# A scan mixer laid out by channel halves in place of even and odd rows

## The chip, the cores and the metric

The kernel runs on one core of a Trainium2 chip, as one launch. The metric is the device time of a whole execution in microseconds, given as the median of several runs; lower is better. A separate execution of the same kernel was profiled, and every busy time, wait and start below is from that one.

## The reference

The input is 32 images of 56 × 56 tokens of 96 channels. Two layers follow one another. Layer 0 adds shifted-window attention (7 × 7 windows, 3 heads) and then a feed-forward product in fp8 (96 → 384 → 96). Layer 1 adds a gated scan along the width and then a second feed-forward product. The change is in the scan mixer of layer 1, which computes this:

```python
x_n   = layernorm(layernorm_c(x))                   # 96 channels
u     = x_n @ W_expand                              # 192 channels
gate  = sigmoid(x_n @ W_gate)                       # 192 channels
# along the width w, for each row and channel e:
state = state * A + u[w] * B                        # 16 states
y[w]  = sum(state * C) + 16 * u[w] * D
out   = x + (gate * y) @ W_out                      # 192 -> 96
```

The recurrence is linear with constant coefficients, so for one channel `y = T_e u`, where `T_e` is a 56 × 56 lower triangular Toeplitz matrix of the channel's taps. The kernel computes the taps once, lays the 192 matrices out in SBUF, and then does the scan as matrix products.

## The kernel before

**Tiles and rounds.** An image is four blocks of 14 rows; a block is 7 tiles (`G`) of two rows, so 112 tokens. A block passes through about a hundred named steps, each an instruction or a few on one engine. The function `pipeline` is written out at build time: in round `t` it goes through a table such as `PIPELINED`, and an entry `name:lag` issues step `name` for block `t - lag`. So about eleven blocks are in flight, and the order of instructions on each engine is exactly the order of the table; every engine runs its own in order. There are three tables: `FILL` for the first 7 rounds, `PIPELINED`, and `DRAIN` for the last ones. The steps `SC` and `GA` work on whole images and are issued in every fourth round only.

**Steps by engine.** TensorE: `q`, `k`, `v` (projections), `sc` (scores), `av` (attention output), `tro`, `pr` (its output projection), `ta`, `tf`, `te`, `tg` (transposes of normalized tiles), `hf0..2`, `yf`, `hg0..2`, `yg` (feed-forward), and of the mixer `pu0..3`, `SC0..5`, `gt0..1`, `so`. VectorE: statistics and normalizations (`s*`, `n*`), `st*` (score scaling), `rc`, `ad`, `as`, `rf*`, `rg*`, `c*`, and `GA0..5`. ScalarE: copies out of PSUM (`e*`, `x*`, `z*`), the exponentials `ex0..2`, `th0..3` and `uc0..3`. GpSimd: the powers `p*`, `k*`, `cf1`, `cg1` and `r0`. SyncE: loads `LD` and stores `ST`. All PSUM tiles come from one pool of four tiles of two banks each, so the fifth tile waits until the first has been read out.

**The mixer before.** The scan needs the position along the width on the partitions. Step `xe` (line 810) writes the transposed tile into `xs`, 96 channels by three rows of 64 columns; `r0` (line 820) copies the first row to the third place. `pu` (lines 831 and 832) takes two rows at once as the stationary operand, 128 columns, so that the even row's tokens come out on partitions 0 to 63 and the odd row's on 64 to 127. It streams 288 columns of the weights over rows 0 and 1, and the last 96 over rows 1 and 2, which puts the second half of the expanded channels on the other half of the partitions. `th` (line 839) writes half the argument's tanh into `gts`, `uc` (line 844) the expanded values into `u`; both hold 128 partitions × 28 row pairs × 192 channels.

`SC` (line 855) multiplies: for each channel and each parity one product of a 64 × 64 piece of `toep` with the 28 rows of that parity of the image. Four such products of 64 × 64 use the four quarters of the array. A step makes 64 of them, `UNIT` = 16 channels of either half, and there are six steps an image. `GA` (line 870) forms (gate + 1) × y into `gts`. `gt` (lines 887 and 893) transposes back, channels on partitions: 128 channels into `gTa`, and the other 64 into the lower or upper half of `gTb` by the tile's parity; `eg` (line 904) copies them out of PSUM. `so` (lines 912 and 916) does the output product: 7 products over 128 channels and 7 over 64.

**Set-up.** `taps_t` holds the taps, position by channel. `load_toep` writes them 56 times to DRAM and reads them back with a slanted pattern, which gives the Toeplitz matrices with position outermost; both halves of the partitions get all 192 channels, in the buffers `gts`. `turn_toep` (line 309) turns them to channel outermost in `toep`, two copies on VectorE and two on ScalarE, before round `gates`, the lag of `th`.

A condition on the inputs picks between this pipeline and a careful, unpipelined one (`IN_TURN`); the inputs here take the pipeline.

Of the kernel before, what the change touches and what calls it, by code (L numbers as in the profile page):

```python
# [23 lines left out]
C = 96  # L24
HW = 56
# [8 lines left out]
UNIT = 16  # L34
# [4 lines left out]
NRP = NBLK * G  # L39
# [17 lines left out]
    "q:2 SC4:8 pf:3 rg2:10 xg1:10 k:2 nf:3 GA3:8 GA4:8 rg1:10 eq:2 pe:4 hg0:10 ne:4 v:2 SC2:8 cg1:10 "  # L57
    "cg2:10 xg0:10 ek:2 ev:2 tf:3 rg0:10 ef:3 so:9 cg0:10 GA2:8 te:4 sc:2 as:9 xe:4 st1:2 st2:2 ST:11 "
    "r0:4 hf2:3 st0:2 xf2:3 ex1:2 ex2:2 yg:10 zg:10 hf1:3 ex0:2 xf1:3 sg:9 SC0:8 pg:9 rf2:3 bg:10 "
    "GA0:8 pu0:4 th0:4 hf0:3 rf1:3 SC5:8 LD:0 uc0:4 cf1:3 pu1:4 ng:9 GA5:8 av:2 xf0:3 rc:2 pa:1 rf0:3 "  # L60
    "uc1:4 th1:4 gt0:8 eg0:8 tg:9 cf0:3 pu2:4 tro:2 pu3:4 kg:10 cf2:3 eg:9 yf:3 uc2:4 th2:4 sa:0 eo:2 "
    "uc3:4 pr:2 zf:3 na:1 bf:3 th3:4 SC1:7 ad:2 ta:1 GA1:7 gt1:8 hg2:9 ea:1 sf:2 kf:3 eg1:8 hg1:9 "
    "SC3:7 xg2:9 se:3 "
# [4 lines left out]
    "GA0:8 pf:3 q:2 bg:10 eq:2 rg2:10 k:2 v:2 cg0:10 yg:10 pe:4 ek:2 xg2:9 hg2:9 nf:3 tf:3 ev:2 "  # L68
    "rg1:10 ne:4 pa:1 gt0:8 xg0:10 zg:10 sc:2 ng:9 ef:3 eg1:8 eg0:8 st1:2 st2:2 kg:10 eg:9 te:4 hf0:3 "
    "st0:2 hf2:3 so:9 xe:4 xf2:3 ST:11 gt1:8 SC4:8 ex0:2 rf2:3 ex1:2 LD:0 cf2:3 r0:4 ex2:2 pu0:4 "  # L70
    "GA3:8 hf1:3 SC1:7 xg1:10 xf0:3 hg0:10 pu1:4 rf0:3 xf1:3 uc1:4 rf1:3 av:2 tg:9 rg0:10 th0:4 pg:9 "
    "rc:2 uc0:4 GA2:8 cf1:3 th1:4 SC5:8 pu2:4 as:9 tro:2 uc2:4 eo:2 cf0:3 GA5:8 yf:3 GA1:7 na:1 zf:3 "
    "sg:9 pr:2 cg2:10 sa:0 SC2:8 bf:3 GA4:8 ad:2 SC0:8 cg1:10 sf:2 kf:3 hg1:9 th2:4 se:3 SC3:7 pu3:4 "
    "ta:1 uc3:4 ea:1 th3:4 "
# [3 lines left out]
    "pf:3 pe:4 hg0:10 rc:2 nf:3 GA3:8 tf:3 k:2 sf:2 rg2:10 ST:11 ne:4 cg2:10 ex2:2 SC5:8 xg1:10 so:9 "  # L78
    "xg0:10 ef:3 SC2:8 hf1:3 eq:2 rg1:10 cg1:10 te:4 tro:2 rg0:10 cg0:10 LD:0 as:9 xf1:3 xe:4 hf2:3 "
    "r0:4 ea:1 hf0:3 yg:10 st1:2 v:2 ek:2 pr:2 xf2:3 GA5:8 pu3:4 xf0:3 sg:9 ev:2 rf1:3 SC4:8 st0:2 "  # L80
    "st2:2 pu1:4 rf2:3 zg:10 rf0:3 cf0:3 pu0:4 th3:4 th1:4 cf2:3 ad:2 ex1:2 cf1:3 uc1:4 GA2:8 GA4:8 "
    "bg:10 q:2 eo:2 ta:1 SC0:8 uc3:4 uc0:4 pg:9 ng:9 th0:4 GA0:8 yf:3 kg:10 pu2:4 zf:3 gt0:8 uc2:4 "
    "av:2 eg0:8 th2:4 ex0:2 bf:3 tg:9 SC1:7 eg:9 pa:1 sc:2 gt1:8 hg2:9 SC3:7 GA1:7 eg1:8 kf:3 hg1:9 "
    "xg2:9 na:1 se:3 sa:0 "
# [5 lines left out]
    "yf:0 zf:0 bf:0 kf:0 se:0 pe:0 ne:0 te:0 xe:0 r0:0 pu0:0 th0:0 uc0:0 pu1:0 th1:0 uc1:0 pu2:0 th2:0 "  # L90
# [7 lines left out]
def kernel(  # L98
# [73 lines left out]
    weg = zeros(2 * E, "weg")  # L172

# [23 lines left out]

    u = const.tile([128, NRP, E], F32, name="u")
    gts = [const.tile([128, NRP, E], F32, name=f"gt_{n}") for n in range(2)]
    for gt, eng in zip(gts, (nc.vector, nc.gpsimd)):  # L200
        eng.memset(gt, 0.0)
# [76 lines left out]
    nc.vector.tensor_copy(taps_t, pt[0 : 2 * HW, 0, 0:E])  # L278
# [3 lines left out]
    toep = const.tile([128, E * HW + RS - HW], F32, name="toep")  # L282
    nc.vector.memset(toep[:, E * HW :], 0.0)

    def load_toep():


        nc.sync.dma_start(taps_d.rearrange("w j e -> j w e"), taps_t[:, None, :].to_broadcast([2 * HW, HW, E]))
        src = taps_d[:, :, :]
        for half in (0, RS):  # L290

            for w0, w1 in ((0, 48), (48, HW - SH), (HW - SH, HW)):
                for t0, t1 in ((0, NRP), (NRP, HW - SH), (HW - SH, HW)):
                    w_in, w_out = (w0 + SH) % HW, (t0 + SH) % HW
                    first = w_in * 2 * HW + HW - w_in + w_out
                    nc.sync.dma_start(
                        gts[t0 // NRP][half + w0 : half + w1, t0 % NRP : t0 % NRP + t1 - t0].rearrange("w t e -> w (t e)"),
                        bass.AP(
                            tensor=src.tensor,
                            offset=src.offset + first * E,  # L300
                            ap=[[(2 * HW - 1) * E, w1 - w0], [1, (t1 - t0) * E]],
                        ),
                    )

    def turn_toep():
        toep3 = toep[:, 0 : E * HW].rearrange("p (e t) -> p e t", t=HW)
        for e0 in range(0, E, EH):
            for n, copy in enumerate((nc.vector.tensor_copy, nc.scalar.copy)):
                copy(
                    toep3[:, e0 : e0 + EH, n * NRP : (n + 1) * NRP],  # L310
                    gts[n][:, :, e0 : e0 + EH].rearrange("p t e -> p e t"),
                )
# [90 lines left out]
    nc.scalar.dma_start(weg[0:C, 0:E], w_gate)  # L403
    nc.scalar.dma_start(weg[0:C, E : 2 * E], w_expand)
    nc.scalar.dma_start(wso[:, 0], ssm_w_out[0:128])
    for p0 in (0, 64):
        nc.scalar.dma_start(wso[p0 : p0 + 64, 1], ssm_w_out[128:E])


    xws, vs, xqs = [], [], []  # L410
# [12 lines left out]
    gTa = const.tile([128, G, TP], F32, name="gTa")  # L423
    gTb = const.tile([128, (G + 1) // 2, TP], F32, name="gTb")
# [10 lines left out]
    xs = const.tile([128, G, 3, RS], F32, name="xs")  # L435
# [372 lines left out]
    def _(i):  # L808
        for g0, g1, pt in held.pop(("tre", i)):
            nc.scalar.activation(  # L810
                xs[0:C, g0:g1, 0:2, 0:HW],
# [6 lines left out]
    @steps("r0")  # L818
    def _(i):
        nc.gpsimd.tensor_copy(xs[0:C, :, 2, 0:HW], xs[0:C, :, 0, 0:HW])  # L820

    def rows_of(i, j):

        return (i % NBLK) * G + 2 * j, min(2, G - 2 * j)

    @steps("pu0", "pu1", "pu2", "pu3")
    def _(i, j):
        pu = banks(f"pu_{i}_{j}")
        for g in range(rows_of(i, j)[1]):
            rows = xs[:, 2 * j + g].rearrange("c r w -> c (r w)")  # L830
            nc.tensor.matmul(pu[:, g, 0 : E + EH], rows[:, 0:128], weg[:, 0 : E + EH], start=True, stop=True)  # L831
            nc.tensor.matmul(pu[:, g, E + EH : 2 * E], rows[:, RS:], weg[:, E + EH :], start=True, stop=True)  # L832
        held["pu", i, j] = pu

    @steps("th0", "th1", "th2", "th3")
    def _(i, j):
        rp, n = rows_of(i, j)
        gt = gts[i // NBLK % 2]
        nc.scalar.activation(gt[:, rp : rp + n, :], held["pu", i, j][:, 0:n, 0:E], AF.Tanh, scale=0.5)  # L839

    @steps("uc0", "uc1", "uc2", "uc3")
    def _(i, j):
        rp, n = rows_of(i, j)
        nc.scalar.copy(u[:, rp : rp + n, :], held["pu", i, j][:, 0:n, E : 2 * E])  # L844
# [3 lines left out]
    def _(n, s):  # L848
        py = banks(f"scan_{n}_{s}")
        for e in range(UNIT):  # L850
            for p in range(2):
                for eh in range(2):
                    ch = eh * EH + s * UNIT + e
                    o0 = (1 - p if eh else p) * RS
                    nc.tensor.matmul(  # L855
                        py[o0 : o0 + RS, eh, e * NRP : (e + 1) * NRP],
                        toep[p * RS : (p + 1) * RS, ch * HW : ch * HW + RS],
                        u[p * RS : (p + 1) * RS, :, ch],
# [6 lines left out]
    def _(n, s):  # L865
        py = held.pop(("scan", n, s))
        for eh in range(2):
            e0 = eh * EH + s * UNIT
# [5 lines left out]
                py[:, eh, 0 : UNIT * NRP].rearrange("p (e q) -> p q e", q=NRP),  # L874
# [7 lines left out]
    def _(i, k):  # L882
        g0, g1 = halves[k]
        gt = gts[i // NBLK % 2][:, i % NBLK * G : (i % NBLK + 1) * G, :]
        pt = banks(f"gt_{i}_{k}")
        for g in range(g0, g1):
            nc.tensor.transpose(pt[:, 0, (g - g0) * 128 : (g - g0 + 1) * 128], gt[:, g, 0:128], ident)  # L887


        for half in (1, 0):  # L890
            for m in range(2):
                g = min(g0 + 2 * m + half, G - 1)
                nc.tensor.transpose(  # L893
                    pt[0 : 64 + 64 * half, 1, m * 128 : (m + 1) * 128], gt[:, g, 128 - 64 * half : E], ident
                )
# [3 lines left out]
    def _(i, k):  # L899
        g0, g1 = halves[k]  # L900
        pt = held.pop(("gt", i, k)).rearrange("c b (s w) -> c b s w", w=RS)[:, :, :, 0:HW]
        for b, dst in ((0, gTa[:, g0:g1]), (1, gTb[:, 2 * k : 2 * k + 2])):
            dst = dst.rearrange("c g (r w) -> c (g r) w", w=HW)
            nc.scalar.copy(dst, pt[:, b, 0 : dst.shape[1]])  # L904

    @steps("so")
    def _(i):
        po = banks(f"so_{i}")[0:TP]
        dst = lambda g: po[:, g % 2, g // 2 * C : (g // 2 + 1) * C]

        for g in range(G):
            nc.tensor.matmul(dst(g), gTa[:, g, :], wso[:, 0, :], start=(g < 2), stop=False)  # L912

        for g in range(G):
            half = slice(g % 2 * 64, g % 2 * 64 + 64)
            nc.tensor.matmul(dst(g), gTb[half, g // 2, :], wso[half, 1, :], start=False, stop=(g >= G - 2))  # L916
        held["so", i] = []
        for b in range(2):
            n = (G + 1 - b) // 2
# [92 lines left out]
```

## Time and profile before

| | |
|---|---|
| median of 3 runs (3761.55 to 3764.2) | 3763.2 us |
| profiled execution, its own time | 3752.4 us |
| its span | 3750.7 us |
| mean granted TensorE clock | 0.984 |
| scan products, `SC` L855: records, mean duration of one | 24576, 221 ns |
| `pu` L831: records, mean duration of one | 1792, 421 ns |
| `pu` L832: records, mean duration of one | 1792, 261 ns |
| `GA` L870 on VectorE: instructions, mean duration of one | 384, 617 ns |

The page gives the busy time of an engine as the union of its instructions; since matrix products overlap in the array, the mean duration of one says little of what it costs, and the distance between starts says more. Each f32 product appears as two records, each with its own load of weights (PEld). The chain of waits is followed back from the last instruction; the chain between two times gives the pieces of it in that stretch. A row of the timeline merges instructions of one kind that follow one another.

### The profile page before, as it was taken

Reading aid. Unit: us, or ns where it says so; the run is one execution under the profiler, and the core shown is the slowest. Engines: PE = TensorE matmul, PEld = TensorE weight load, DVE = VectorE, ACT = ScalarE, POOL = GpSimd, SP = SyncE. Lnnn points to the kernel's source line nnn. Section 1 sums busy time; section 2 is a strip of 40 time slices with the busy share of each in tenths; the row PEclk is TensorE's granted clock in tenths of the full one; section 3 lists DMA queues with packets and bytes.
Section 4 is the critical chain, followed back from the end, with each engine's and each line's share of the span. In section 5 each row is a group of like instructions: output and inputs, shape, how many; then the busy total and the mean of one; then the engine's idle time right before and its main releaser. Section 6 shows DMA issues by size and latency. Waiting matters only on the chain.

```text
span 3750.7 us, 179098 instructions
## 1 busy us (share of the span) xinstructions
PE 3623.0 (97%) x78756; PEld 3079.2 (82%) x78756; DVE 3140.3 (84%) x9418; ACT 2327.9 (62%) x4867; POOL 1427.9 (38%) x1176
## 2 busy tenths in 40 slices
PE   4999999999999999999999999999999999999996
PEld 3788888888888888888888888888888888888875
DVE  5788888888888888888888888888888888888875
ACT  2666666666666666656666666666666666666662
POOL 2333333443334443334443434443334443334432
PEclk8999999999999999999999999999999999999997
DMA  6001011011001101100101101101011101101000
GB/s 137 17 13 26 23 23 29 22 25 26 22 23 26 25 23 27 23 23 23 29 22 27 24 23 25 26 22 29 23 23 26 25 22 28 23 23 26 22 15 22
DMA packets 226367, 99.42 MB, mean 27 GB/s; under 512 B 218492, under 2 KB 225246, under 8 KB 225358
## 3 DMA queue, kind: packets, MB, share of 16 engines
q1 hardware_dynamic: 222522, 86.81, 10.4%
q8 instruction: 623, 10.21, 1.1%
q10 hardware_dynamic: 3060, 1.08, 0.1%
q14 instruction: 162, 1.33, 0.1%
HBM read 44.47 MB, written 43.35 MB: 23 GB/s over the span
## 4 chain that ended last, share of the span: by engine, by line
PE 94%; DMA 2%; issue 2%; DVE 2%; POOL 1%; ACT 0%; SPq 0%; ACTq 0%; POOLq 0%; DVEq 0%
PE pu L831 12%; PE scan L855 11%; PE qk L550 8%; PE av L674 5%; PE pv L569 5%; PE so L912 5%; PE pr L723 5%; PE pu L832 5%; PE s L592 4%; PE ph_g L743 4%; PE ph_f L743 4%; PE py_f L777 4%; PE py_g L777 3%; PE so L916 3%; PE gt L887 3%; PE tr_o L703 3%
## 5 line engine op out<-in xcount | busy, mean ns | idle before, releaser
L831 PE MATMUL pu<-weg,xs 128*128 128x288 f32 x1792 | 608.5, 421 | 2.4 <-ACT h_f L755 1.2
L799 POOL TENSOR_TENSOR xb<-xb,y_f 112x672 f32<-112x672 f32 x128 | 188.0, 1469 | 782.7 <-DVE y_f L795 782.7
L855 PEld LDWEIGHTS scan<-u,toep 64*64 64x64 f32 x24576 | 385.4, 136 | 83.9 <-issue 59.1
L855 PE MATMUL scan<-u,toep 64*64 64x28 f32 x24576 | 411.0, 221 | 21.4 <-issue 20.3
L832 PEld LDWEIGHTS pu<-weg,xs 128*128 128x128 f32 x1792 | 340.3, 190 | 96.1 <-POOL xs L820 1.9
L755 ACT CAST h_g<-ph_g 128x784 f16<-128x784 f32 x384 | 302.6, 837 | 122.7 <-PE ph_g L743 112.4
L755 ACT CAST h_f<-ph_f 128x784 f16<-128x784 f32 x384 | 316.9, 827 | 76.4 <-PE ph_f L743 70.2
L623 DVE SCALAR_TENSOR_TENSOR pT<-s,bias 128x392 f32<-128x392 f32 (+1 forms) x512 | 213.6, 459 | 142.3 <-PE s L592 137.9
L810 ACT ACTIVATE xs<-tr_e,bet,gam 96x448 f32<-96x448 f32 (+1 forms) x256 | 158.6, 668 | 269.3 <-PE tr_e L499 269.3
L474 POOL TENSOR_TENSOR rs_g<-rs_g,neg_half 112x7 f32<-112x7 f32 x128 | 202.9, 1585 | 319.8 <-DVE rs_g L468 319.8
L870 DVE SCALAR_TENSOR_TENSOR gt<-gt,scan 128x448 f32<-128x448 f32 x384 | 220.9, 617 | 121.5 <-PE scan L855 121.5
L820 POOL COPY xs<-xs 96x392 f32<-96x392 f32 x128 | 65.7, 513 | 673.7 <-issue 662.5
L550 PE MATMUL qk<-xw,wqkv 128*32 128x196 f32 (+1 forms) x3072 | 310.8, 398 | 11.8 <-ACT xw L540 7.6
L832 PE MATMUL pu<-weg,xs 128*128 128x96 f32 x1792 | 320.9, 261 | 0.5 <-POOL xs L820 0.4
L484 DVE TENSOR_SCALAR xn_g<-xb,st_g,rs_g 112x96 fp8e5<-112x96 f32 x896 | 295.6, 397 | 30.2 <-POOL rs_g L474 30.1
L844 ACT COPY u<-pu 128x384 f32<-128x384 f32 (+1 forms) x512 | 233.1, 456 | 115.5 <-PE scan L855 59.9
L831 PEld LDWEIGHTS pu<-weg,xs 128*128 128x128 f32 x1792 | 281.9, 191 | 19.5 <-ACT h_f L755 2.0
L484 DVE TENSOR_SCALAR xn_e<-xb,st_e,rs_e 112x96 f32<-112x96 f32 x896 | 287.9, 390 | 0.2 <-POOL rs_e L474 0.2
L839 ACT ACTIVATE gt<-pu 128x384 f32<-128x384 f32 (+1 forms) x512 | 242.8, 474 | 56.1 <-PE pu L832 56.1
L474 POOL TENSOR_TENSOR rs_f<-rs_f,neg_half 112x7 f32<-112x7 f32 x128 | 201.1, 1571 | 183.4 <-DVE rs_f L468 183.4
L550 PEld LDWEIGHTS qk<-xw,wqkv 128*32 128x32 f32 (+1 forms) x3072 | 117.6, 119 | 165.3 <-issue 69.2
L904 ACT COPY gTa<-gt 128x448 f32<-128x448 f32 (+1 forms) x256 | 125.3, 490 | 193.9 <-PE gt L893 183.7
(151 smaller groups left out, 9015.2 us busy)
## 6 DMA issues: line engine op xcount, KB each, us to landing
xb<-in_x_dram SPq DMA_DIRECT2D x224, 126.0 KB
out_dram<-xb SPq DMA_DIRECT2D x224, 126.0 KB
taps_d<-u SPq DMA_DIRECT2D x1, 4704.0 KB
xb<-in_x_dram SPq DMA_DIRECT2D x224, 13.1 KB
xb<-in_x_dram SPq DMA_DIRECT2D x224, 7.9 KB
out_dram<-xb SPq DMA_DIRECT2D x224, 13.1 KB
out_dram<-xb SPq DMA_DIRECT2D x224, 7.9 KB
xb<-in_x_dram SPq DMA_DIRECT2D x32, 72.0 KB
```

Source lines behind the costliest of these rows:

```text
L474: nc.gpsimd.tensor_tensor(rs, rs, neg_half, ALU.pow)
L484: nc.vector.tensor_scalar(xn[:, g, :], xb[:, g, :], mean[:, col], rs[:, col], op0=ALU.subtract, op1=ALU.mult, **saturate)
L550: nc.tensor.matmul(pq[j * rows : (j + 1) * rows, m, 0:size], wqkv[:, m * C + h0 * HD : m * C + h1 * HD], xws[i % 2][:, j * size : (j + 1) ...
L743: nc.tensor.matmul(ph[:, half, 0:HALF], w1q[:, hc * 128 : (hc + 1) * 128], xqs[layer][:, half * HALF : (half + 1) * HALF], start=True, sto ...
L755: nc.scalar.copy(h16.rearrange("p (h t) -> p h t", h=2), held.pop(("ph", n, i, hc))[:, :, 0:HALF])
L777: nc.tensor.matmul(po[:, g - g0, :], hq[hc][:, g * TP : (g + 1) * TP], w2q[:, hc, :], start=(hc == 0), stop=(hc == 2),)
L831: nc.tensor.matmul(pu[:, g, 0 : E + EH], rows[:, 0:128], weg[:, 0 : E + EH], start=True, stop=True)
L832: nc.tensor.matmul(pu[:, g, E + EH : 2 * E], rows[:, RS:], weg[:, E + EH :], start=True, stop=True)
L839: nc.scalar.activation(gt[:, rp : rp + n, :], held["pu", i, j][:, 0:n, 0:E], AF.Tanh, scale=0.5)
L844: nc.scalar.copy(u[:, rp : rp + n, :], held["pu", i, j][:, 0:n, E : 2 * E])
L855: nc.tensor.matmul(py[o0 : o0 + RS, eh, e * NRP : (e + 1) * NRP], toep[p * RS : (p + 1) * RS, ch * HW : ch * HW + RS], u[p * RS : (p + 1) ...
L870: nc.vector.scalar_tensor_tensor(part, part, 1.0, py[:, eh, 0 : UNIT * NRP].rearrange("p (e q) -> p q e", q=NRP), op0=ALU.add, op1=ALU.mult,)
```

## The change

The mixer's partitions no longer stand for the row's parity. Every row comes out on both halves of the partitions, and each half holds half of the channels.

- `xs` has two rows in place of three and `r0` is gone. `weg` is arranged in two halves of 192 columns: gate and expansion of 96 channels each. The two halves of the expansion have 48 of their channels swapped, which replaces the third row.
- `pu` takes one row as the stationary operand, 64 columns, and streams 192 columns, once for either half of the partitions: 4 products for a tile where there were 2.
- `u` and `gts` hold 128 partitions × 56 rows × 96 channels. A scan product has all 56 rows of an image as its moving columns; a step has 32 products of 64 × 64, with `UNIT` = 8.
- `toep` holds 96 channels on either half, half its former size. The slanted read takes pieces of 96 channels, all into `gts[1]`; the turn is one copy on VectorE and one on ScalarE, and it stands one round later. `taps_t` is copied in four pieces in swapped order.
- `gt` is one transpose for a row, 128 × 96; `eg` is one copy for each of two buffers `gT_0` and `gT_1`; `so` is two products over 96 channels (of 128 rows, the others zero) for each tile, 14 in all.
- All three tables are new. In `PIPELINED` the orders of the TensorE steps are:

```
before  q SC4 k hg0 v SC2 tf so te sc hf2 yg hf1 SC0 pu0 hf0 SC5 pu1 av gt0 tg pu2 tro pu3 yf pr SC1 ta gt1 hg2 hg1 SC3
after   te yg hf1 hf2 SC5 pu1 SC0 pu0 av gt0 tg pu2 tro pu3 yf pr hg2 ta gt1 hg0 SC3 SC1 hg1 SC2 q k SC4 v so tf sc hf0
```

The longest lag falls from 11 to 10 (`ST`). The head of the new ScalarE order is xf0, xe, zg, xf1, ex1, ex0, ex2; that of VectorE is st1, st0, st2, sg, rf0, bg, rf1, ng, GA5, GA0. The core of the diff:

```diff
-UNIT = 16
+UNIT = 8
-    u = const.tile([128, NRP, E], F32, name="u")
-    gts = [const.tile([128, NRP, E], F32, name=f"gt_{n}") for n in range(2)]
-    for gt, eng in zip(gts, (nc.vector, nc.gpsimd)):
-        eng.memset(gt, 0.0)
+    u = const.tile([128, HW, EH], F32, name="u")
+    gts = [const.tile([128, HW, EH], F32, name=f"gt_{n}") for n in range(2)]
+    nc.gpsimd.memset(gts[1], 0.0)
...
-    nc.vector.tensor_copy(taps_t, pt[0 : 2 * HW, 0, 0:E])
+    ne = EH // 2
+    for e0, src in ((0, 0), (ne, 3 * ne), (2 * ne, 2 * ne), (3 * ne, ne)):
+        nc.vector.tensor_copy(taps_t[:, e0 : e0 + ne], pt[0 : 2 * HW, 0, src : src + ne])
...
-        for half in (0, RS):
+        for half in range(2):
...
-                            ap=[[(2 * HW - 1) * E, w1 - w0], [1, (t1 - t0) * E]],
+                            offset=src.offset + first * E + half * EH,
+                            ap=[[(2 * HW - 1) * E, w1 - w0], [E, t1 - t0], [1, EH]],
...
+        for e0, copy in ((0, nc.vector.tensor_copy), (EH // 2, nc.scalar.copy)):
+            part = slice(e0, e0 + EH // 2)
+            copy(toep3[:, part, :], gts[1][:, :, part].rearrange("p t e -> p e t"))
...
+    for h in range(2):
+        own, other = h * EH, (1 - h) * EH + ne
+        nc.scalar.dma_start(weg[0:C, h, 0:EH], w_gate[:, own : own + EH])
+        nc.scalar.dma_start(weg[0:C, h, EH : EH + ne], w_expand[:, own : own + ne])
+        nc.scalar.dma_start(weg[0:C, h, EH + ne : E], w_expand[:, other : other + ne])
...
+        gT = const.tile([128, 2, 8 - 2 * n, HW], F32, name=f"gT_{n}")
+        nc.vector.memset(gT[C:], 0.0)
...
-    @steps("r0")
-    def _(i):
-        nc.gpsimd.tensor_copy(xs[0:C, :, 2, 0:HW], xs[0:C, :, 0, 0:HW])
...
-        for g in range(rows_of(i, j)[1]):
-            rows = xs[:, 2 * j + g].rearrange("c r w -> c (r w)")
-            nc.tensor.matmul(pu[:, g, 0 : E + EH], rows[:, 0:128], weg[:, 0 : E + EH], start=True, stop=True)
-            nc.tensor.matmul(pu[:, g, E + EH : 2 * E], rows[:, RS:], weg[:, E + EH :], start=True, stop=True)
+        for g in range(tiles_of(i, j)[0]):
+            for r in range(2):
+                for h in range(2):
+                    nc.tensor.matmul(
+                        pu[h * RS : (h + 1) * RS, g, r * E : (r + 1) * E],
+                        xs[:, 2 * j + g, r, :],
+                        weg[:, h, :],
+                        start=True,
+                        stop=True,
+                    )
...
-            for p in range(2):
-                for eh in range(2):
-                    ch = eh * EH + s * UNIT + e
-                    o0 = (1 - p if eh else p) * RS
+            for b in range(2):
+                ch = b * EH // 2 + s * UNIT + e
+                for h in range(2):
+                    o0 = (h ^ b) * RS
                     nc.tensor.matmul(
-                        py[o0 : o0 + RS, eh, e * NRP : (e + 1) * NRP],
-                        toep[p * RS : (p + 1) * RS, ch * HW : ch * HW + RS],
-                        u[p * RS : (p + 1) * RS, :, ch],
+                        py[o0 : o0 + RS, b, e * HW : (e + 1) * HW],
+                        toep[h * RS : (h + 1) * RS, ch * HW : ch * HW + RS],
+                        u[h * RS : (h + 1) * RS, :, ch],
...
-                py[:, eh, 0 : UNIT * NRP].rearrange("p (e q) -> p q e", q=NRP),
+                py[:, b, 0 : UNIT * HW].rearrange("p (e q) -> p q e", q=HW),
...
+        for r in range(2 * (g1 - g0)):
+            nc.tensor.transpose(
+                pt[0:C, r // 4, (r % 4) * 128 : (r % 4 + 1) * 128],
+                gts[i // NBLK % 2][:, (i % NBLK * G + g0) * 2 + r, :],
+                ident,
+            )
...
+        nc.scalar.copy(gTs[k][0:C], pt[:, :, 0:rows, 0:HW])
...
-        for g in range(G):
-            nc.tensor.matmul(dst(g), gTa[:, g, :], wso[:, 0, :], start=(g < 2), stop=False)
-        for g in range(G):
-            half = slice(g % 2 * 64, g % 2 * 64 + 64)
-            nc.tensor.matmul(dst(g), gTb[half, g // 2, :], wso[half, 1, :], start=False, stop=(g >= G - 2))
+        for gT, (g0, g1, po) in zip(gTs, out_banks(f"so_{i}")):
+            for g in range(g1 - g0):
+                for h in range(2):
+                    token = gT[:, h, 2 * g : 2 * g + 2, :].rearrange("c r w -> c (r w)")
+                    nc.tensor.matmul(po[:, g, :], token, wso[:, h, :], start=(h == 0), stop=(h == 1))
...
-            if t == gates:
+            if t == gates + 1:
                 turn_toep()
```

## The prediction

> **What bounds the kernel now.** I read the page first: busy time by engine, then the 40 slices.
>
> ```profile
> PE 3623.0 (97%) x78756; PEld 3079.2 (82%) x78756; DVE 3140.3 (84%) x9418; ACT 2327.9 (62%) x4867; POOL 1427.9 (38%) x1176
> PE   4999999999999999999999999999999999999996
> PEclk8999999999999999999999999999999999999997
> PE 94%; DMA 2%; issue 2%; DVE 2%; POOL 1%; ACT 0%; SPq 0%; ACTq 0%; POOLq 0%; DVEq 0%
> ```
>
> TensorE is busy at full clock in every slice but the ends, and 94% of the chain of waits is TensorE's. Next the chain between 600 and 3400 us, 100 rounds of 28.0 us, 25 images of 112.0 us:
>
> ```profile
> by line: PE pu L831 12.9%; PE scan L855 11.0%; PE qk L550 8.2%; PE av L674 5.4%; PE pv L569 5.3%; PE so L912 5.1%; PE pr L723 5.0%; PE pu L832 4.8%; PE s L592 4.5%; PE ph_f L743 4.1%; PE ph_g L743 3.9%; PE py_g L777 3.8%; PE py_f L777 3.8%;
> ```
>
> So `pu` (two lines, 17.7%) costs 4.96 us a round, the scan 3.1. Then the sums over two rounds, one without and one with scans (each row: length, then busy time of PE, PEld, DVE, ACT, POOL):
>
> ```profile
> 1914.54:1939.16 24.62, 24.62 (x424) 20.82 (x424) 22.55 (x71) 17.97 (x39) 11.03 (x9) 1.00 0.12 27
> 1865.14:1901.42 36.28, 35.63 (x1065) 30.87 (x1066) 28.39 (x80) 18.40 (x38) 9.65 (x8) 1.00 0.09 21
> ```
>
> TensorE has no idle time in the plain round; VectorE follows at 92%. Scans cost an image 112.0 − 4 × 24.62 = 13.5 us. Last, for prices, the timeline and the chain in single rounds (start, length; a group's cost is the distance to the next start):
>
> ```profile
> 1954.98 0.51 PE L743 MATMUL ph_g<-xq,w1q 128*128 128x392 fp8e5 x2
> 1955.42 1.54 PE L569 MATMUL pv<-wqkv,xw 128*64 128x96 f32 x32
> 1956.89 0.55 PE L497 MATMUL tr_f<-ident,xn_f 112*96 112x112 fp8e5 x7
> 1957.27 1.57 PE L912 MATMUL so<-wso,gTa 128*112 128x96 f32 x14
> 1958.77 1.02 PE L916 MATMUL so<-wso,gTb 64*112 64x96 f32 x14
> 1959.73 0.49 PE L499 MATMUL tr_e<-ident,xn_e 112*96 112x112 f32 x3
> ...
> 1914.54 0.48 PE pu L831 x2
> 1917.65 1.53 PE av L674 x96
> 1863.14 2.00 PE scan L855 x128
> 1865.14 0.81 PE tr_a L499 x7
> ```
>
> An f32 product is two records. From these rows:
> - Streaming: `pu` at 288 columns takes 0.48 us for two records, 0.83 ns a column and record.
> - Two 64-column halves run side by side: `pv` (128*64, 96 columns) has 32 records of 80 ns, 2.56 us one at a time, but takes 1.47, so 16 pairs of 80 ns plus about 0.19.
> - Four 64*64 tiles: 24 sets of `av` take 1.53 us, 32 of the scan 2.00. The difference is 0.47/8 = 58.8 ns a set and 0.12 fixed. 33 columns are no dearer than 28: the 64 weight columns set the pace.
> - A visit to a split array costs about 0.28 us beyond its work: `ph_g` lasts 0.44 us before `pv` and 0.33 elsewhere (+0.1), `pv` has 0.15 of start and drain, the next group 0.04.
>
> [...] the trace has 58.8 a set and 1.41/14 = 101 for `so`[...].
>
> **The change part by part** (per round unless said otherwise).
>
> *Scan.* Half the products, 56 columns in place of 28. Streaming is 56 × 0.83 = 46.7 ns, below the 58.8 of the loads, so a set of four should cost the same and a step has 16 sets, not 32: 0.94 + 0.12 = 1.06 us. With the delay of what follows (tr_a 0.81 us in place of 0.67) and the switches next to `pu` and hg, which the new table interleaves with scans, I take 1.1 a step, 6.6 us an image: −6.9 of 13.5. Unknown: whether load and stream still overlap when nearly equal. If not, a set is 58.8 + 46.7 = 105 ns and a step 1.8, 10.8 an image. From below, nothing here undercuts the load pace.
>
> *`pu`.* 14 products of 128 weight columns and 288 or 96 moving ones become 28 of 64 and 192, on two halves. Side by side: 28 pairs of records × 162.5 (160 and the 2.5 that `pv`'s 82.5 spacing has over 80) = 4.55. They stand in three visits (pu1+pu0, pu2, pu3): + 3 × 0.28 = 0.84, less 0.10 for the switch into `av` that exists already: 5.29 against 4.96, **+0.33**. If the halves took turns it would be 4.55 more.
>
> *`so`.* Today 14 records at 128 rows (1.41), 14 row-paired ones (0.95), and 0.13 on the transpose after them, 2.49. Now 28 at 100 ns, 2.80: **+0.31**. *`gt`.* 15 transposes become 14, and the first after `av` has 96 weight columns, not 128: **−0.12**. *Order.* The k product goes straight to `pv`, not through hg0: one drain and re-entry less, **−0.15**.
>
> Sum: +0.37 a round, 1.5 us an image; with the scan −5.4 us, × 32 = **−173 us**.
>
> *ScalarE and VectorE.* Gate, copy and product move as many elements (384, 384, 448); the two gate copies-out become one of 896 and one of 672 elements in place of 448, 336 and twice 224: by the 784-element row (813 to 837 ns) about 1.65 us against 0.53 + 0.45 + 2 × 0.36 = 1.70, nothing. The product reads runs of 8 where it had 16; no row shows that; I take 0, bounds −0.1 to +0.6 us each, beside TensorE unless VectorE becomes late. *POOL.* The row copy (0.51) goes; it waited for nothing and held nobody in the steady rounds: 0. The SP queue issues its loads at the head of the round and stores in the middle; the 11 buffers now have a lag of 10, not 11, so no load should wait: 0. If that failed, the first layer norm would be late, and VectorE behind it.
>
> *New waits.* The round is now dense at its head. In a plain round `ex2` on ScalarE stands behind xf0, xe, zg, xf1 and two exponentials: 0.25 to start, then 0.83 + 1.34 + 0.87 + 0.79 + 1.5 = 5.6 us, while TensorE gets to `av` after 0.68 + 1.09 + 0.66 + 2.75 + 0.1 = 5.3. So `av` waits some 0.3, three rounds of four, and everything on TensorE behind it. In the scan round `gt0` needs GA5 and GA0, which VectorE ends at about 9.3 us, when TensorE arrives: close to 0. I charge **+1.0 us an image, 32 us**; bounds 0 and 4.
>
> *Ends.* The table's turning is half: ScalarE's two copies (9.59 us) held TensorE twice, 3.41 and 3.91 us, near 93 and 99 us. One stays, a round later and with the scan still two rounds away: −5. The 4.54 us memset at the head of VectorE goes, two smaller ones and three table copies come: −2. The gather is 2.4 MB in 384-byte pieces where it was 4.8 MB in long ones: hidden, since it gains a round. **−7.**
>
> The profiled execution took 3752.4 us with a span of 3750.7; 3752 − 173 + 32 − 7 = 3604. The median of the three runs lies 10.8 above that execution, so I add about as much, less a little as the fall may scale: **3612 us**.
>
> **The rivals.**
> 1. *Forecast:* TensorE still bounds and the scan's loads set its pace. 3575 (no new waits) to 3660. Chance 0.66.
> 2. *VectorE and ScalarE come late often.* VectorE needs 3 × 22.55 + 28.4 = 96 us an image, 90% of the new 107.6. For: `av` and `gt0` above. Against: at 92% in plain rounds it keeps up today without idle time on TensorE. With 3.5 us of waits an image: 3612 + 80 = 3692. Chance 0.16.
> 3. *The scan gains little*, load and stream in turn: + 4.2 × 32 = 134, 3746; half of it, 3680. For: both are nearly equal now. [...] Chance 0.06.
> 4. *Slower:* the halves of `pu` take turns, as both read the same 128 rows. Price 4.55 × 128 = 582, 4194. It decides once a pair takes over 162.5 + 151/(128 × 28) = 205 ns in place of 162.5. For: no row pairs 192 columns, and here both halves load the same weights. Against: `pv` and q, both 128*64. Chance 0.12, with room for a combined failure of order and pace.
>
> **How the numbers follow.** Likeliest 3612, its own range 3575 to 3660. For 8 in 10 I leave out rival 4 and the far part of rival 3: 3550 (visits to the split array 0.1 us cheaper each, less than nothing waited) to 3705. A measurement of this kernel tells 0.2%, about 8 us, from no change. Faster: 0.66 + 0.16 + 0.04 = 0.86; same 0.02; slower 0.12.
>
> **What would show it.** Scan records halved and a step near 1.1 us; `pu` near 5.3 and `so` near 2.8 us a round; a plain round of about 25.2 us, 0.3 of it waiting before `av` on the exponential; VectorE busy time unchanged at 24 us a round. I am wrong if a pair of `pu` takes over 200 ns, a scan set over 70, or if TensorE idles over 1 us a round on VectorE.

## The result, and the profile after

| | before | after |
|---|---|---|
| median | 3762.4 us (3760.9 to 3764.2, 4 runs) | 3712.8 us (3711.2 to 3713.8, 4 runs) |
| span of the profiled execution | 3750.7 us | 3709.1 us |
| records of the scan, mean of one | 24576, 221 ns | half as many, 273 ns |
| an image in the middle of the run | 112.64 us | 111.94 us |
| its four rounds | 31.9, 24.6, 24.6, 31.5 us | 28.96, 25.38, 25.38, 32.22 us |

The ratio is 0.9868, with an interval of 0.985 to 0.9885: faster by 1.3%, where 4% was forecast. An image is the distance between the starts of `pv` four blocks apart, the mean of 25 images; the prediction took 112.0 for it in the kernel before.

From the page of the kernel after, the lines that answer to those of before (busy time and share by engine; then the chain that ended last):

```profile
PE 3595.0 (97%) x69924; PEld 2974.7 (80%) x69924; DVE 3320.5 (90%) x9421; ACT 2338.5 (63%) x4610; POOL 1423.3 (38%) x1048
...
PE 77%; DVE 17%; ACT 3%; POOL 1%; issue 1%; DVEq 0%; ACTq 0%; POOLq 0%
```

There are 8832 fewer records on TensorE (12288 of the scan went, others came), and yet it is as busy a share of the span as before. VectorE has got 180 us busier, and part of the chain now runs over it. The chain between 600 and 3400 us, by line:

```profile
by line: PE pu L830 16.1%; PE scan L862 9.1%; PE so L914 8.1%; PE qk L550 6.3%; PE gt L893 5.0%; PE av L674 4.9%; PE pv L569 4.1%; PE pr L723 3.9%; PE py_g L777 3.9%; PE py_f L777 3.9%; PE s L592 3.5%; PE tr_o L703 3.2%; PE ph_f L743 3.0%; 
```

The scan still holds 9.1%, against 11.0%, with half its products. Two rounds of the kernel after, a scan round and a plain one (time, length, then busy time of PE, PEld, DVE, ACT, POOL):

```profile
1958.32:1987.26 28.94, 28.71 (x581) 23.75 (x582) 24.76 (x71) 17.81 (x35) 9.42 (x7) 1.00 0.10 24
1987.26:2012.62 25.36, 25.14 (x453) 20.70 (x454) 24.23 (x71) 18.07 (x37) 11.04 (x9) 1.00 0.07 16
```

TensorE idles 0.2 us in each. The plain round is 0.78 us longer than before, near the forecast (0.37 of work and 0.3 of waiting). So most of the miss lies with the scan. What an image has beyond four plain rounds was 112.6 − 4 × 24.6 = 14.2 us before (13.5 in the prediction, from its 112.0) and is 111.94 − 4 × 25.38 = 10.4 now; 6.6 was forecast. The chain of the kernel after in single steps (start, length, what):

```profile
1932.12 0.45 PE ph_f L743 x2
1932.57 0.02 issue
1932.59 0.82 ACT h_f L755
1933.41 0.04 issue
1933.45 1.24 PE py_g L777 x21
...
1952.62 1.72 PE scan L862 x64
1954.34 2.27 PE qk L550 x24
1956.60 1.72 PE scan L862 x64
```

A step of 64 records takes 1.72 us, 26.9 ns a record; the 128 records of before took 2.00 us, 15.6 each. With the fixed 0.12, a set (one record on each of the four tiles) takes about 1.6/16 = 100 ns, not 58.8 (99 from start to start). The first lines are the new wait: `py_g` waits for the copy of `ph_f` out of its PSUM tile.

Between 600 and 3400 us TensorE is without work for 22 us in the kernel before and for 22.6 in the kernel after, but in different places. Its waits (total, times, longest), the longest entry of before and then both of after:

```profile
PE scan L855 <- issue: 13.3, 18, 1.2
...
PE py_g L777 <- ACT h_f L755: 15.1, 67, 0.2
PE py_g L777 <- DVE pT L623: 7.5, 33, 0.2
```

Before, most of it lay inside scan steps, where the profile shows nothing that TensorE waited for. Six times in this stretch, about 1 us or less after an idle time of 0.8 to 1.4 us, the kernel before was also granted only half the clock for 3.4 us; one of the six (the third number from the end is the granted clock):

```profile
746.10:749.40 3.30, 3.30 (x23) 3.26 (x21) 1.15 (x2) 0.86 (x2) 0.00 (x0) 0.50 0.02 5
```

The kernel after has no such stretch between 114 and 3580 us. Half of 6 × 3.4 us over 25 images is 0.4 us an image, an estimate, and more than half of the 0.69 us by which an image got shorter. The work itself got only about 0.3 us an image shorter: what the scan saves goes nearly all to the plain rounds. What makes the idle times inside the scan isn't shown.

### The profile page after: what moved, and what is told of

Its sections match the earlier page's. It is cut to its first block, busy times and chain, and to the rows that moved or that the text cites. A ratio compares the mean times of both kernels' runs of the same rounds, so it can differ in the third digit from the quotient of the medians.

```text
span 3709.1 us, 160788 instructions
## 1 busy us (share of the span) xinstructions
PE 3595.0 (97%) x69924; PEld 2974.7 (80%) x69924; DVE 3320.5 (90%) x9421; ACT 2338.5 (63%) x4610; POOL 1423.3 (38%) x1048
## 4 chain that ended last, share of the span: by engine, by line
PE 77%; DVE 17%; ACT 3%; POOL 1%; issue 1%; DVEq 0%; ACTq 0%; POOLq 0%
PE pu L830 15%; PE scan L862 9%; PE so L914 8%; PE qk L550 6%; PE gt L893 5%; PE av L674 4%; PE pv L569 4%; PE pr L723 4%; PE py_f L777 4%; PE py_g L777 4%; PE s L592 3%; PE tr_o L703 3%; PE ph_f L743 3%; PE ph_g L743 3%; DVE xn_f L484 2%; DVE pT L623 2%
## 5 line engine op out<-in xcount | busy, mean ns | idle before, releaser
L830 PE MATMUL pu<-weg,xs 128*64 128x192 f32 x7168 | 675.7, 333 | 0.0
L830 PEld LDWEIGHTS pu<-weg,xs 128*64 128x64 f32 x7168 | 479.4, 137 | 125.0 <-ACT u L850 21.3
L474 POOL TENSOR_TENSOR rs_a<-rs_a,neg_half 112x7 f32<-112x7 f32 x128 | 197.0, 1539 | 579.3 <-DVE rs_a L468 579.3
L914 PE MATMUL so<-wso,gT 128*112 128x96 f32 x3584 | 384.0, 265 | 0.1
L914 PEld LDWEIGHTS so<-wso,gT 128*112 128x112 f32 x3584 | 363.9, 179 | 16.2 <-ACT h_g L755 1.7
L484 DVE TENSOR_SCALAR xn_a<-xb,st_a,rs_a 112x96 f32<-112x96 f32 x896 | 361.3, 471 | 0.2 <-POOL rs_a L474 0.2
L484 DVE TENSOR_SCALAR xn_f<-xb,st_f,rs_f 112x96 fp8e5<-112x96 f32 x896 | 344.8, 452 | 3.6 <-POOL rs_f L474 3.6
L862 PE MATMUL scan<-u,toep 64*64 64x56 f32 x12288 | 336.0, 273 | 0.0
L904 ACT COPY gT<-gt 96x896 f32<-96x896 f32 (+1 forms) x256 | 209.2, 817 | 139.5 <-PE gt L893 126.2
L893 PE MATMUL gt<-ident,gt 128*96 128x128 f32 x1792 | 245.1, 277 | 1.4 <-DVE gt L877 1.4
```

What stands on the lines that cost most here:

```text
L474: nc.gpsimd.tensor_tensor(rs, rs, neg_half, ALU.pow)
L484: nc.vector.tensor_scalar(xn[:, g, :], xb[:, g, :], mean[:, col], rs[:, col], op0=ALU.subtract, op1=ALU.mult, **saturate)
L830: nc.tensor.matmul(pu[h * RS : (h + 1) * RS, g, r * E : (r + 1) * E], xs[:, 2 * j + g, r, :], weg[:, h, :], start=True, stop=True,)
L862: nc.tensor.matmul(py[o0 : o0 + RS, b, e * HW : (e + 1) * HW], toep[h * RS : (h + 1) * RS, ch * HW : ch * HW + RS], u[h * RS : (h + 1) * R ...
L893: nc.tensor.transpose(pt[0:C, r // 4, (r % 4) * 128 : (r % 4 + 1) * 128], gts[i // NBLK % 2][:, (i % NBLK * G + g0) * 2 + r, :], ident,)
L914: nc.tensor.matmul(po[:, g, :], token, wso[:, h, :], start=(h == 0), stop=(h == 1))
```

## The experiments

The set of about 100 ns is close to what the third rival had (105), and its reason there was that load and stream run in turn. Two other reasons offered themselves: the order of the products, which now goes over the row halves innermost, and how the moving columns are read. Channel `ch` of `u[:, :, ch]` is one f32 in every 96, so a column comes every 384 bytes; before, one in every 192, so every 768.

**The order of the products.** The loops as before, row half outermost:

```diff
-            for b in range(2):
-                ch = b * EH // 2 + s * UNIT + e
-                for h in range(2):
+            for h in range(2):
+                for b in range(2):
+                    ch = b * EH // 2 + s * UNIT + e
```

> The changed kernel with the four scan products of a set in the order of the kernel before (both column halves of the lower rows first). A set of four takes 98 ns in the changed kernel. Theory A (the moving columns are read at a stride of 384 bytes and stream at half pace, 2 x 46.7 + 5 ns): no difference, a set stays at 98 ns, a step of 64 records near 1.72 us, time within 5 us of the changed kernel. Rival B (loads don't overlap streams when the row half alternates from product to product): a set falls to about 59 ns, a step to 1.06 us, the time by about 6 x 0.6 x 32 = 115 us at most.

Measured: 3710.9 us in one run. A step in its chain of waits:

```profile
1970.74 1.71 PE scan L862 x64
```

The order of the products makes no difference.

**The moving columns read without gaps.** The 56 columns stand next to each other:

```diff
+        uf = u.rearrange("p t e -> p (t e)")
-                        u[h * RS : (h + 1) * RS, :, ch],
+                        uf[h * RS : (h + 1) * RS, ch * HW : (ch + 1) * HW],
```

> The changed kernel with the moving operand of the scan product read from 56 adjacent elements of the same buffer, in place of one element in each 96; the scan therefore works on other values, all else is the same. Theory A (stride): a set of four falls from 98 to 59 ns (the pace of the weight loads), a step from 1.72 to about 1.1 us, the time by 3 to 3.7 us an image, 95 to 120 us, if VectorE (103 us of 112 an image) doesn't take over, else less. Rivals B (order) and C (four tiles can't stream at once at full pace): a set stays at 98 ns, time unchanged.

Measured: 3609.9 us in one run, 103 us less than after, and an image of 108.64 us. Its chain of waits:

```profile
1904.39 1.08 PE scan L863 x64
```

Products, loads and columns are as many as in the kernel after. Only the addresses of the moving columns differ, and the step takes the 1.06 to 1.1 us that the sum had, although TensorE now idles for 9.5 us between 600 and 3400 us inside scan steps, as it did in the kernel before (the mean granted clock here was 0.989, as in the kernel after). Load and stream overlap also at 46.7 beside 58.8 ns, so the third rival's mechanism falls.

**The same with the right values.** `u` itself with the channel outermost, so that the copy `uc` writes with gaps and the scan reads without:

```diff
-    u = const.tile([128, HW, EH], F32, name="u")
+    u = const.tile([128, EH, HW], F32, name="u")
-        nc.scalar.copy(by_tile(u[:, rows, :]), held["pu", i, j][:, 0:n, :, EH:])
+        nc.scalar.copy(by_tile(u[:, :, rows].rearrange("p e t -> p t e")), held["pu", i, j][:, 0:n, :, EH:])
-                        u[h * RS : (h + 1) * RS, :, ch],
+                        u[h * RS : (h + 1) * RS, ch, :],
```

> The changed kernel with the buffer u held channel outermost, so that a scan product reads its 56 columns from adjacent elements and the result is the reference's; the copy uc on ScalarE writes at a stride of 224 bytes instead. Theory A: a set near 59 ns as in the run with the contiguous read, and the same time as that run, some 3600 to 3640 us, if the strided write costs ScalarE nothing (0.50 us for 384 elements). If the strided write doubles uc (+1.7 us a round on ScalarE at 18 of 28 us) up to half of the gain is lost before av. Rivals B and C: no change, 3713.

Measured: 3609.0 us (3607.5 to 3610.9, 4 runs), ratio to before 0.9582 (0.9566 to 0.9598). Groups of instructions by shape between 600 and 3400 us (count, then busy time and mean ns of one, then idle time before), first of the kernel after:

```profile
L862 PE MATMUL scan<-u,toep 64*64 64x56 f32 x9600 | 263.0, 273 | 0.0
```

and of this one:

```profile
L862 PE MATMUL scan<-u,toep 64*64 64x56 f32 x9728 | 173.3, 220 | 9.6 <-issue 9.6
...
L850 ACT COPY u<-pu 128x384 f32<-128x384 f32 x309 | 263.9, 920 | 24.2 <-PE pu L830 13.7 <-PE scan L862 10.4
```

The records fall from 273 to 220 ns, to the 221 that they had before the change. The price goes to ScalarE, whose copy takes 920 ns in place of 497, and there it is hidden: the rounds are 27.73, 25.38, 25.38 and 30.19 us, the plain ones unchanged to the hundredth.

**The old tables.** The kernel after with the three tables of before, `r0` struck out:

```diff
 PIPELINED = (
-    "te:4 st1:2 LD:0 st0:2 xf0:3 yg:10 xe:4 st2:2 hf1:3 zg:10 hf2:3 sg:9 SC5:8 rf0:3 pu1:4 xf1:3 pg:9 "
...
+    "q:2 SC4:8 pf:3 rg2:10 xg1:10 k:2 nf:3 GA3:8 GA4:8 rg1:10 eq:2 pe:4 hg0:10 ne:4 v:2 SC2:8 cg1:10 "
...
```

> The changed kernel with the three tables of the kernel before, less the entry of the row copy. If the layout alone decides (TensorE bound, sum of its pieces), the time lies within 20 us of the changed kernel: 4 visits more to the split array, as pu stands in four places (pu0, pu1 between full-array products), 1 more re-entry at 0.28 us a round each, against 0.4 us a round less waiting at yg: 3710 to 3760. If the new tables bring the gain of the ends (one lag less, some 17 us) and of the order, 3730 to 3780. If the new tables cost VectorE its time (xn_a and xn_f at 460 to 480 ns beside GpSimd in place of 325), VectorE busy falls back to about 24.2 us a round here.

Measured: 3709.1 us (3707.7 to 3709.7, 4 runs), ratio 0.9846 (0.983 to 0.9863); an image of 111.97 us. Sums between 600 and 3400 us (length, then busy time of PE, PEld, DVE, ACT, POOL), first of the kernel after:

```profile
600.00:3400.00 2800.00, 2777.39 (x54622) 2304.82 (x54621) 2581.45 (x7303) 1822.67 (x3603) 1106.89 (x801) 1.00 0.11 24
```

and with the old tables:

```profile
600.00:3400.00 2800.00, 2799.84 (x54612) 2271.98 (x54609) 2419.43 (x7302) 1820.68 (x3603) 1051.18 (x800) 1.00 0.11 24
```

The new tables' 22.6 us without work on TensorE are gone, VectorE is 162 us less busy, and the image is as long as with the new tables to 0.03 us. What waited is now worked, in more visits to the split array: a round's `pu` takes 5.17 us from start to start where the new table has 5.05, and `ph_f` and `ph_g` together 0.18 more. So with this scan neither the new waits nor VectorE's extra load is a loss that the old order would give back; the layout decides, as the first of the forecasts had it. Where VectorE's time comes from is seen in its groups of the same stretch; the kernel after:

```profile
L484 DVE TENSOR_SCALAR xn_a<-xb,st_a,rs_a 112x96 f32<-112x96 f32 x703 | 292.8, 484 | 0.0
L484 DVE TENSOR_SCALAR xn_f<-xb,st_f,rs_f 112x96 fp8e5<-112x96 f32 x700 | 274.5, 459 | 0.0
```

and with the old tables:

```profile
L484 DVE TENSOR_SCALAR xn_f<-xb,st_f,rs_f 112x96 fp8e5<-112x96 f32 x700 | 176.7, 324 | 8.0
L484 DVE TENSOR_SCALAR xn_a<-xb,st_a,rs_a 112x96 f32<-112x96 f32 x700 | 175.9, 323 | 0.0
```

The same instructions on the same tiles have means 135 to 160 ns higher in the new order. But no single one takes 0.46 or 0.48 us: of the seven in such a group six take 0.32, and one is long. A piece of the timeline of the kernel after shows it (start, length, engine):

```profile
1986.43 1.72 POOL L474 TENSOR_TENSOR rs_e<-rs_e,neg_half 112x7 f32<-112x7 f32 x1
1987.55 1.46 DVE L484 TENSOR_SCALAR xn_f<-xb,st_f,rs_f 112x96 fp8e5<-112x96 f32 x1
...
1988.11 0.83 POOL L767 CAST hq_g<-h_g 128x784 fp8e5<-128x784 f16 x1
```

The long one ends 0.07 us after GpSimd's cast. So it is in the traces of both kernels, before and after: two of the 28 normalizations of a round are long, and all of them between 600 and 3400 us (199 and 200) end 0.06 to 0.07 us after a GpSimd instruction of line 767 or 799. In the kernel before, which has the old order, they stand in `xn_e` and `xn_g` and take 0.82 to 0.89 us; in the kernel after most take 1.46 to 1.48. With the old tables here `xn_e` and `xn_g` have means of 393 and 392 ns, where the kernel before has 394 and 391. It isn't GpSimd at work as such: in the kernel before 990 of the short ones run wholly beside another GpSimd instruction (line 474). That they take longer makes about 110 of the 162 us; most of the rest lies in VectorE's part of the cast `hq_f`. That GpSimd holds VectorE fits all of this, but no run moved its work alone.

**Both together.** The channel outermost in `u` and the old tables:

> The changed kernel with both edits: the tables of the kernel before (less the row copy) and u channel outermost. With the old tables TensorE never idles (2799.8 of 2800 us), so the time is the sum of its pieces: plain round 25.38 as in both, scan 7.1 an image as in the run with channel-major u, 108.6 an image and 3600 to 3612 us. If VectorE (24.2 us a round in the old order against 25.8) was what held the new tables back, it is faster: below 3595.

Measured: 3597.4 us (3595.4 to 3598.2, 4 runs), ratio 0.9543 (0.9515 to 0.9571), image 108.42 us. This lies between the two forecasts. The intervals of this and of the new tables with the same `u` overlap slightly, so their order isn't settled by the times; in the profiled executions the old tables are 0.27 us an image shorter, and TensorE idles 3 us in 2800 where the new tables have 34.

**Did the gaps cost anything before?** The kernel before, its 28 columns read without gaps:

```diff
+        uf = u.rearrange("p t e -> p (t e)")
-                        u[p * RS : (p + 1) * RS, :, ch],
+                        uf[p * RS : (p + 1) * RS, ch * NRP : (ch + 1) * NRP],
```

> The kernel before, with its 28 moving columns of the scan read from adjacent elements in place of one in 192; the scan works on other values. Theory A (a strided column costs double, 2 x 23.3 + 5 = 52 ns, which hides behind the weight loads' 58.5): a set stays at 58.5 ns and the time at 3750 to 3765. If the stride had cost anything before, a set falls below 55 ns and the time by 20 us or more.

Measured: 3768.2 us in one run, beside 3765.0 for the kernel before itself on the same chip. Its chain of waits:

```profile
1983.56 2.00 PE scan L856 x128
```

No gain: the step is as long as with the gaps. That fits a stream that at 28 columns stays below the 58.8 ns of the loads even in its slow form (47 ns, estimated below), and then the trace before could not show the slow pace. It also speaks against gaps that stop load and stream from overlapping: a set of the kernel before would then take about 58.8 + 23.3 = 82 ns.

**Where the gap begins.** The kernel after, with 56 columns at a distance of 2 elements, 8 bytes, and in a second kernel of 4 elements, 16 bytes:

```diff
+        uf = u.rearrange("p t e -> p (t e)")
+                o1 = min(ch * HW, (EH - 2) * HW)
-                        u[h * RS : (h + 1) * RS, :, ch],
+                        uf[h * RS : (h + 1) * RS, o1 : o1 + 2 * HW : 2],
```

> The changed kernel with its 56 moving columns at a stride of two elements (8 bytes) of the same buffer, the scan on other values. [...] full pace: a set near 59 ns, about 3610 us. If any step but one costs double: 98 ns, 3711 us.

> As the run with stride two, with a stride of four elements (16 bytes)[...]. [...] half pace again, a set at 98 ns and about 3711 us, as at 384 bytes. If the price grows with the distance, something between 59 and 98 ns, 3620 to 3690 us.

Measured: 3608.7 us at 8 bytes, 3725.8 us at 16 bytes, one run each. The chain at 8 bytes:

```profile
1904.72 1.08 PE scan L864 x64
```

and at 16 bytes:

```profile
1976.00 1.80 PE scan L864 x64
```

8 bytes cost nothing that shows beside the loads, 16 as much as 384, or a little more. So at 8 bytes the stream still hides behind the loads, and at 16 it doesn't. A distance of 12 bytes wasn't tried, and why the border lies there isn't shown. A step of 16 sets goes from 1.08 to between 1.72 and 1.80 us; a set, with 56 columns on each tile, then takes 99 to 105 ns, where 2 × 46.7 = 93 would be half pace. Half pace for 28 columns gives 2 × 23.3 = 47 ns, an estimate from the same row, and that lies below the 58.8 of the loads, as the kernel before needs it.

**Fewer visits to the split array.** Since only TensorE's own work is left in the last version, a full-array step that splits a visit should be worth moving. Of the old order, `hf0` stands between `pu0` and `pu1`, and `hg0` between k and `pv`. First both moved:

```diff
-... pe:4 hg0:10 ne:4 v:2 SC2:8 ... hf1:3 ex0:2 ... th0:4 hf0:3 rf1:3 ...
+... pe:4 ne:4 v:2 hg0:10 SC2:8 ... hf1:3 hf0:3 ex0:2 ... th0:4 rf1:3 ...
```

> As the run with both edits, and in the steady table hf0 stands before pu0 (so pu0 and pu1 are one visit to the split array in plain rounds) and hg0 after v (so the k product goes straight to pv). At 0.28 us a visit and 0.15 to 0.2 for the second, a plain round falls from 25.4 to about 24.95, and the time by 50 to 60 us below the run with both edits, to about 3550. If a wait for a PSUM tile or for the exponentials takes its place, less, or slower.

Measured: 3623.2 us (3620.0 to 3624.3, 4 runs), ratio 0.961 (0.9582 to 0.9638): slower than without the moves. The waits of TensorE between 600 and 3400 us (total, times, longest):

```profile
PE so L908 <- ACT h_g L749: 42.7, 77, 0.6
```

`hg0` has come so close to `so` that `so` finds its PSUM tile still being read by the copy of `h_g`, 0.55 us each time. Then `hf0` alone:

> Of the two moves of the run with fewer visits only hf0 before pu0; hg0 stays between k and v. In that run TensorE waited before so for ScalarE's copy of hg0, 0.55 us a plain round, where the kernel with both edits waits for nothing. If the move of hg0 alone made this wait, it goes, and the saved visit (0.28 us in the plain rounds, 64 to 96 of 128) brings the time 18 to 30 us below the 3597 of the run with both edits. If the denser head of the round costs too (av behind the exponentials), no gain.

Measured: 3570.5 us (3569.5 to 3572.6, 4 runs), ratio 0.9474 (0.9458 to 0.9489). Its sums between 600 and 3400 us:

```profile
600.00:3400.00 2800.00, 2796.81 (x56913) 2296.54 (x56915) 2513.93 (x7601) 2003.71 (x3750) 1092.12 (x832) 1.00 0.11 25
```

TensorE idles 3 us in 2800, and a plain round takes 25.13 us in place of 25.38: one visit less, 0.25 us, where the prediction priced a visit at 0.28. The two last kernels differ only in the place of `hg0`, with plain rounds of 25.76 and 25.13 us. The wait is 0.55 of these 0.63, so letting the k product go straight to `pv`, which the prediction priced at 0.15, saves nothing here. Of the kernels run, this is the fastest.

## Why the prediction was wrong

- **The scan, the step that failed:** "Streaming is 56 × 0.83 = 46.7 ns, below the 58.8 of the loads, so a set of four should cost the same". The 0.83 ns came from `pu`, whose moving operand lies without gaps. The scan's columns come 384 bytes apart and stream at about half that pace, so the stream, not the load, sets the set's time: 99 ns from start to start, a step of 1.72 us where 1.1 was forecast. The scan saved 14.2 − 10.4 = 3.8 us an image where 6.9 was forecast. That is 3.1 × 32 = 99 us of the 107 between 3604 and the profiled execution's 3711. Taking the gaps away, and nothing else, takes off 103 us and gives 3609 to 3610. That this is so near the 3612 of the forecast is in part luck, since the misses on the plain rounds and on the ends nearly cancel.
- **The third rival** had the size, 105 ns a set and 10.8 us an image (99 and 10.4 measured), with the wrong mechanism: load and stream do run side by side. It got 0.06 because only the overlap was asked about, not whether the pace of the stream carried over to this operand.
- **The plain round:** +0.78, so 3.1 us an image, where 1.5 of work and 1.0 of waiting were forecast: 0.6 × 32 = 20 us too little. In it `so` came to 2.83 us (2.80 forecast), and `pu` to 5.05 from start to start (5.29), with part of the cost of its visits falling on the neighbours. The halves of `pu` work side by side, so the fourth rival is out.
- **The new wait** came, but elsewhere: before `yg`, on a PSUM tile that the copies of `h_f` and `pT` still read, 22.6 us in 100 rounds, and not before `av` on the exponentials. With the old order it goes and, with this scan, nothing is won.
- **"VectorE busy time unchanged at 24 us a round"** was wrong: 25.8 in the kernel after. The prediction counted elements; two normalizations a round are longer still in the new order (most 1.46 to 1.48 us, beside 0.82 to 0.89), each ending 0.06 to 0.07 us after a GpSimd instruction. The second rival still fails, since TensorE's waits on VectorE are 7.5 us in 2800 and VectorE's 24.2 us a round with the old tables bring no time.
- **The ends** gave more than the 7 us forecast. The span fell by 41.6 us, and the image's 0.69 times 32 accounts for 22, which leaves about 19. From the first `pv` to the fifteenth it is 352.3 us in place of 366.8, and the tail after the last `pv` 154.8 in place of 158.2. In the first of these TensorE idled 24.1 us in place of 31.1, which is about what was forecast, and had half the clock for 27.3 us in place of 41.0, worth some 7 us more (an estimate, half of the difference). The clock had no place in the sum. Which part of the set-up brought either wasn't tried.

In sum: 99 from the scan and some 20 from the plain rounds, less 12 from the ends, the 107.

## What to carry to other kernels

A pace is only as good as the operand that it was read from: before a duration of one row is used for another, compare the distance between its elements too, and ask whether the slower form could have been hidden in the kernel before (here by the weight loads). When a product is made wider to save weight loads, lay its moving columns next to each other and let the copy that writes them carry the gaps, on an engine that has room. Before moving steps together to save visits to a split array, look at which PSUM tile the next step needs and who still reads it: one of two such moves won 0.7%, the other lost more than that.

## What the runs showed of the hardware

- f32 moving columns 16 or 384 bytes apart stream at about half pace (set of four 64 × 64 tiles, 56 columns: 99 to 105 ns); 4 or 8 bytes apart a step of 16 sets takes 1.08 us. A set takes 58 ns from start to start with 28 columns (the scan before) and with 33 (`av`); that the loads of the weights set this pace is inferred from that. With 28 columns, 768 and 4 bytes make no difference (a step of 32 sets in 2.00 us).
- ScalarE's copy of 384 f32 out of PSUM takes 0.50 us when it writes runs of 96, and 0.92 us when every element goes 224 bytes from the last.
- VectorE's normalization of 112 × 96 f32 takes 0.32 us, but two of 28 a round take 0.82 to 1.48 us and end 0.06 to 0.07 us after a GpSimd instruction of line 767 or 799. That GpSimd holds them is inferred from the times.
- In the kernel before, TensorE was granted half the clock for 3.4 us six times between 600 and 3400 us, each time about 1 us or less after an idle time of 0.8 to 1.4 us. Not every such idle time is followed by this: of 18 of 0.76 to 1.39 us in this stretch, the clock stayed full after the other twelve.
